# Two side streams of a scan kernel: from a flush at each pair's end to running on across it

## The chip, the cores and the metric

The kernel runs on one core of one Trainium2 chip. The metric is the device time of one execution in microseconds (us), the median of several runs. PE is TensorE, DVE is VectorE, ACT is ScalarE, POOL is GpSimd, SP is SyncE, which here issues all DMAs.

## The reference

64 images of 96 x 28 x 28 go through four layers in sequence.

```python
x = _L0_conv_ref(x, ...)      # expand to 576, depthwise 5x5 with four mixed experts per image, gate, project
x = _L1_conv_ref(x, ...)      # norm, in_proj, 3x3 conv, four-way selective scan, norm, gate, out_proj, MLP
t = _to_tokens(x)
t = t + _L2_attn_ref(_ln_t(t), ...)   # FFT over the 784 tokens, mixing, inverse FFT
t = t + _L2_ffn_ref(_ln_t(t), ...)    # quantised MLP
t = t + _L3_attn_ref(_ln_t(t), ...)
t = t + _L3_ffn_ref(_ln_t(t), ...)
x = _from_tokens(t, x)
```

The part that sets the order of everything is the scan in layer 1. For each of four directions k, 192 channels and 16 states, along 784 positions:

```python
def step(hst, inp):
    dt_t, x_t, B_t, C_t = inp
    dA = jnp.exp(dt_t[..., None] * A[None])
    dBx = dt_t[..., None] * B_t[:, :, None, :] * x_t[..., None]
    hst = hst * dA + dBx
    y_t = jnp.einsum('bkdn,bkn->bkd', hst, C_t)
    return (hst, y_t)
```

## The kernel before

Images are worked in 32 pairs. All that a pair needs falls into three strands, and the program interleaves the strands of neighbouring pairs.

**The scan** is the main strand. A pair has 192 *units*, in 12 blocks of 16. A block is a direction k and a channel tile T (T = 0 and 1: 128 channels of one image; T = 2: the remaining 64 of both). The order of the blocks is (0,0), (2,0), (0,1), (2,1), (0,2), (2,2) and then the same with k = 1 and 3. A unit holds 32 channels by 4 states on 128 partitions, along 784 positions. It consists of:
- `decay`: ACT computes da = exp(dt A), issued four units ahead (AHEAD, L74; the pool of da has 5 buffers);
- `spread_b`: PE spreads four rows of B to pb in PSUM, whenever image or group of states changes (4 times in a block with T = 0 or 1, 8 times with T = 2);
- `recur`: DVE multiplies pb by u to pd (L1045) and scans da and pd to h (L1050 forward, L1052 backward);
- POOL multiplies h by the rows of C (tile cs);
- `collect`: every four units, PE adds the four products into yp; at the end of a forward and backward block pair `keep` copies yp to xy, and SP stores it.

`prepare_block` fetches the next block's B rows (unit 1 of a block) and its dt4 and u4 (units 7 and 9 to 15, five buffers of each name), each spread to 128 partitions by the DMA; `fetch_c` fetches cs three units ahead (three buffers). All of them read DRAM tensors that the first stream wrote.

**Stream a** (`first_half`) is a generator that makes a pair's scan inputs: layer 0, then in_proj and the 3x3 convolution, then for k = 0 and 2 the B and C rows, dt and u, and after that (the point `ready`) the same for k = 1 and 3. **Stream b** (`second_half`) takes a pair's y through the rest of layer 1 and through layers 2 and 3. A generator yields after each *piece*. `yield 0` lets it go on in the same *window*, `yield 1` ends the window. A stream opens at most one window a unit, and `after(n, ...)` puts work off by n windows. Stream a has 131 windows, stream b 153.

The program order is written at build time by `run`. For each unit it writes the scan's instructions and then calls `advance`, which writes pieces of the due streams as long as the planner's clock of PE (`Clocks`, a table of assumed costs) is not past an allowance. That allowance is the planner's clock of DVE plus ROOM (0.3; EARLY, -0.3, where a new pb is two units off), plus GAIN (0.2) times how many windows the stream is behind its plan, plus a catch-up term that grows towards the end of the pair:

```python
late.update({v: v.base + (n + 1 - v.start) * v.rate - v.window for v in streams})      # L1179
advance(due, lambda v: until + GAIN * late[v] + max(0, late[v] - (per - n) / 4))      # L1182
if n == per - 1:
    finish(streams)
```

While the scan of pair p runs, stream a of pair p + 1 goes from unit 0 to unit 191, and stream b of pair p - 1 from unit 6 to unit 191. `finish` writes everything that is left of both after unit 191, without an allowance. So each stream begins and ends with a scan's pair. Each of the two streams has one PSUM bank; where one of them is alone (`alone`, in the first and last pair) it takes both in turn. After the last unit, `finish` writes all of the last pair's stream b. Each engine runs its instructions in the order written.

Of the kernel before, what the change touches and what calls it, by code (L numbers as in the profile page):

```python
# [75 lines left out]


BEFORE, ROOM, EARLY, GAIN, CHOICE = 6, 0.3, -0.3, 0.2, 0.1
WINDOWS = {"a": 131, "b": 153}


class Clocks:
# [107 lines left out]
class Stream:  # L190


    def __init__(self, name, clocks, pieces, rate, start):
        self.name, self.clocks, self.pieces = name, clocks, pieces
        self.window, self.later = 0, {}

        self.base, self.start, self.rate = 0, start, rate
# [27 lines left out]
class Model:  # L225
# [294 lines left out]
    def first_half(self, p, st):  # L520
        nc, act = self.nc, self.act
        after = lambda n, run: self.a_stream.after(n, run)
        dma = nc.sync.dma_start
# [7 lines left out]
        for i, k in enumerate((k0, k1)):  # L531
            t = k[:, : 10 * C]
# [223 lines left out]
        for b in range(2):  # L756
            v = wp[:, 4 * b : 4 * b + 4, :]
# [4 lines left out]
        for b in range(2):  # L762
            for h in range(2):
# [7 lines left out]
                v = xs[b][:, cols(h)]  # L771
# [121 lines left out]
        def project(k):  # L893
            v, s = self.rows_a.tile([128, L], F32, name="o"), stacked[k // 2]
            hi, mid, lo = parts
            for h in range(2):
                pt = bank()
                for T in range(3):
                    self.mm(
                        pt[:100, :HALF], w_p[:, k, T, :], source[T][:, cols(h)], start=(T == 0), stop=(T == 2)  # L900
                    )
                    if T == 1:
                        yield 0
                act(v[:100, cols(h)], pt[:100, :HALF], AF.Copy)
                if h == 0:
                    yield 1

            def placed(i, t):
                dma(st["b"][k][32 * i : 32 * i + 32], t[:32])
                dma(s[36 * i : 36 * i + 36], t[32:68])  # L910

            def second():
                act(mid, v[:68], AF.Copy)

            def third():
                self.gpsimd.tensor_sub(lo, v[:68], mid)
                placed(1, mid)
                placed(2, lo)

            def first():  # L920
                self.gpsimd.tensor_sub(v[:68], v[:68], hi)
                dma(st["c"][k % 2][32 * (k // 2) : 32 * (k // 2) + 32], v[68:100])
                placed(0, hi)

            act(hi, v[:68], AF.Copy)
            after(1, first)
            after(2, second)
            after(3, third)
            yield 1

        def product(k, T, dt, x):
            self.gpsimd.tensor_mul(us[0], dt, x)
            dma(st["dt"][k][T], dt)
            after(1, lambda: dma(st["u"][k][T], us[0]))

        def steps(k):

# [44 lines left out]
    def prepare_block(self, u, at):  # L982

        nc, st, k, T = self.nc, u["st"], u["k"], u["T"]
        if at == 1:
            if u["blk"] in (0, 1, 6, 7):
                self.bs[k] = self.bss.tile([C, L], BF16, name="bsl")
                nc.sync.dma_start(self.bs[k], st["b"][k])
        for name, v, when in (("dt4", "dt", (7, 10, 11, 12)), ("u4", "u", (9, 13, 14, 15))):
            if at in when:  # L990
                j = when.index(at)
                t = self.reps.tile([128, L], F32, name=name)
                self.landed[(u["p"], u["blk"], name, j)] = nc.sync.dma_start(
                    t, st[v][k][T][32 * j : 32 * j + 32, None, :].broadcast_to([32, 4, L])
                )
                self.rep[(u["p"], u["blk"], name, j)] = t

    def fetch_c(self, u):
        b = self.image_of(u)
        t = self.css.tile([128, L], F32, name="cs")  # L1000
        at = 32 * (u["k"] // 2) + 16 * b + 4 * u["g"]
        self.nc.sync.dma_start(t, u["st"]["c"][u["k"] % 2][at : at + 4].partition_broadcast(32))
        self.cs[self.key(u)] = t
# [80 lines left out]

    def run(self):
        nc, act, clocks = self.nc, self.act, self.clocks
        sts = [dict(p=p) for p in range(self.npairs)]
# [5 lines left out]

        fresh = lambda i: 0 < i < len(units) and self.key(units[i]) != self.key(units[i - 1])

        def stream(name, p, start=0):
            pieces = self.first_half if name == "a" else self.second_half
            v = Stream(name, clocks, pieces(p, sts[p]), WINDOWS[name] / (per - 2 - start), start)
            setattr(self, name + "_stream", v)
            return v  # L1100

# [20 lines left out]
        first, setup = stream("a", 0), Stream("b", clocks, self.setup_second(), 1, 0)  # L1122
# [3 lines left out]
        first.base, first.rate = first.window, 1  # L1126
        for at in range(16):
            self.prepare_block(units[0], at)
        self.fetch_c(units[0])
# [2 lines left out]
        decayed = AHEAD  # L1132
        clocks.dve = max(clocks.dve, clocks.pe)
        self.spread_b(units[0])
        streams = [first]
        for i in range(len(units) + 6):
            u = units[i] if i < len(units) else None
            n = i % per

            if u and n == 0:  # L1140
                self.alone = i // per in (0, self.npairs - 1)
            if i < per and first.over and streams == [first]:
                streams = [stream("a", 1, n)]
            elif u and n == 0 and i > 0:
                streams = [stream("a", i // per + 1, n)] if i // per + 1 < self.npairs else []
            elif u and n == 6 and i // per > 0:
                streams.append(stream("b", i // per - 1, n))
            if i % 4 == 2 and 6 <= i < len(units) + 3:
                self.collect(units[i - 6 : i - 2])
            if u:  # L1150
# [37 lines left out]
    def second_half(self, p, st):  # L1188
# [509 lines left out]
```

## Time and profile before

| | |
|---|---|
| median of 3 runs | 22441.52 us (22433.54 to 22450.66) |
| the profiled execution, its own time | 22503.17 us |
| its span, first to last instruction | 22501.5 us |
| mean granted clock of TensorE | 0.832 |
| busy: PE, DVE, ACT, POOL | 77%, 82%, 61%, 71% of the span |
| DMA | 4285.68 MB, 190 GB/s, 62.0% of the 16 engines' span |
| first scan starts, last scan starts | 415.9 us, 22173.4 us |

How to read it: busy times are of one profiled execution. A row of a group gives the line, the engine, the operation, output and inputs, shapes and count; then the busy time in us and the mean of one in ns; then the idle time of the engine just before these instructions and what ended most of it. The granted clock is the share of full speed that TensorE was allowed. L157 is the line of all ACT calls, L253 of all matmuls, L137 of the streams' DVE and POOL calls, so that the tile names tell the pieces apart: `slot` and `bank_b` belong to stream b; `r`, `k`, `t`, `o`, `pad`, `bank_a` to stream a.

### The profile page before, as it was taken

To read this page: it belongs to the slowest core of one execution; us is meant where nothing else is said; L and a number is where in the kernel's file an instruction comes from. 1 tells how busy PE (TensorE), PEld (TensorE's weight loads), DVE (VectorE), ACT (ScalarE), POOL (GpSimd) and SP (SyncE) were. 2 spreads that over 40 slices of the span, in tenths; PEclk is the share of its full clock that TensorE was granted. 3 is DMA by queue.
4 is the path that set the end of the run, shared out by engine and by line. 5 is a ranking of instruction groups with operands and counts; after the bars stand their busy time and mean duration, and the time that the engine had idled before them with its cause. 6 is when DMAs were issued, how large, how long until landed. Compare 5 with 4: busy or idle time off the path is not lost. (4 is left out here: it accounts for less than half of the span.)

```text
span 22501.5 us, 294265 instructions
## 1 busy us (share of the span) xinstructions
PE 17323.6 (77%) x100890; PEld 6770.9 (30%) x100890; DVE 18393.0 (82%) x15290; ACT 13649.8 (61%) x19357; POOL 15987.8 (71%) x9834
## 2 busy tenths in 40 slices
PE   5778777787777777777877777877778777778766
PEld 2233323332323333323323233323233232333222
DVE  2988888888888888888888888888888888888884
ACT  3566666666666666666666666666666666666654
POOL 2777777777777777777777777777777777777774
PEclk8888888888878888888888888888888888888877
DMA  5766666666666666666666666666666666666642
GB/s 155 229 189 197 201 203 187 191 193 200 202 194 187 189 195 198 205 192 192 192 196 200 193 189 197 196 197 200 193 191 190 195 202 193 193 193 190 199 158 63
DMA packets 1764775, 4285.68 MB, mean 190 GB/s; under 512 B 212500, under 2 KB 447084, under 8 KB 1763177
## 3 DMA queue, kind: packets, MB, share of 16 engines
q1 hardware_dynamic: 1763276, 4266.86, 62.0%
q8 instruction: 799, 13.09, 0.2%
q14 instruction: 700, 5.73, 0.1%
HBM read 3207.28 MB, written 882.92 MB: 182 GB/s over the span
## 5 line engine op out<-in xcount | busy, mean ns | idle before, releaser
L137 POOL TENSOR_TENSOR h<-h,cs 128x784 f32<-128x784 f32 x6144 | 11357.7, 1856 | 3875.7 <-DVE h L1050 1175.6
L1045 DVE TENSOR_TENSOR pd<-pb,u 128x784 f32<-128x784 f32 x6144 | 6016.4, 979 | 2346.6 <-PE pb L253 1029.1
L157 ACT ACTIVATE da<-dt,c_A_logs 128x784 f32<-128x784 f32 x6144 | 5661.2, 940 | 2014.4 <-DVE h L1052 865.4
L1052 DVE TENSOR_TENSOR_SCAN h<-da,pd 128x784 f32<-128x784 f32 x3072 | 5487.5, 1786 | 152.9 <-DVE pd L1045 2.8
L1050 DVE TENSOR_TENSOR_SCAN h<-da,pd 128x784 f32<-128x784 f32 x3072 | 5487.4, 1786 | 130.5
L253 PE MATMUL bank_a<-k,t 128*32 128x392 f32 (+1 forms) x37840 | 3984.7, 529 | 204.3 <-ACT pad L157 122.9
L253 PE MATMUL yp<-h,c_gather 128*32 128x512 f32 (+1 forms) x24576 | 3058.3, 595 | 131.3 <-POOL h L137 121.4
L137 POOL TENSOR_TENSOR slot<-slot,slot 96x392 f32<-96x392 f32 (+6 forms) x1700 | 2203.4, 1301 | 1197.3 <-ACT slot L157 988.8
L157 ACT ACTIVATE slot<-bank_b 128x392 f16<-128x392 f32 (+4 forms) x2546 | 1245.4, 489 | 2277.4 <-PE bank_b L253 2235.4
L253 PE MATMUL pb<-bsl,c_sel 96*128 96x512 bf16 (+1 forms) x4096 | 1192.2, 378 | 1320.4 <-DVE pd L1045 1294.1
L253 PEld LDWEIGHTS bank_a<-k,t 128*32 128x32 f32 (+1 forms) x37840 | 1267.2, 116 | 2391.1 <-issue 1894.3
L253 PEld LDWEIGHTS yp<-h,c_gather 128*32 128x32 f32 x24576 | 797.2, 124 | 2472.3 <-issue 2032.4
L253 PE MATMUL bank_b<-slot,c_center 96*128 96x392 f32 x1736 | 955.3, 638 | 396.1 <-DVE slot L137 243.8
L253 PE MATMUL bank_b<-c_fwd,slot 99*96 99x196 f32 (+1 forms) x3968 | 844.7, 359 | 354.1 <-DVE slot L137 254.9
L253 PEld LDWEIGHTS <-c_sel 96*128 96x128 bf16 x4096 | 353.5, 103 | 2469.8 <-issue 1666.9
L157 ACT ACTIVATE o<-bank_a,bn_b,bn_s 128x392 f32<-128x392 f32 x572 | 385.1, 673 | 1113.1 <-PE bank_a L253 1113.1
L157 ACT ACTIVATE slot<-slot 96x786 f32<-96x786 f32 (+5 forms) x1166 | 890.0, 790 | 85.9 <-DMA slot<-in_dt_w 37.6
L253 PEld LDWEIGHTS bank_b<-c_fwd,slot 99*96 99x96 f32 x3968 | 664.9, 175 | 583.4 <-issue 483.1
L157 ACT ACTIVATE slot<-bank_b,c_l_mix 96x393 f32<-96x393 f32 x736 | 446.1, 638 | 632.5 <-PE bank_b L253 418.0
L137 POOL TENSOR_TENSOR k<-k,r 128x784 f32<-128x784 f32 x256 | 472.0, 1844 | 423.1 <-ACT k L157 276.4
L253 PE MATMUL bank_a<-k,cv_diag 96*32 96x392 f32 x4464 | 612.2, 683 | 207.6 <-DMA k<-padded 175.8
L253 PE MATMUL bank_a<-k,k 108*128 108x392 bf16 x744 | 331.2, 445 | 567.5 <-ACT k L157 203.2
(265 smaller groups left out, 20797.5 us busy)
## 6 DMA issues: line engine op xcount, KB each, us to landing
cs<-crow SPq DMA_DIRECT2D x2048, 392.0 KB
dt<-dt SPq DMA_DIRECT2D x1536, 392.0 KB
u<-u SPq DMA_DIRECT2D x1536, 392.0 KB
k<-padded SPq DMA_DIRECT2D x2304, 256.0 KB
padded<-pad SPq DMA_DIRECT2D x384, 592.0 KB
u<-k SPq DMA_DIRECT2D x384, 392.0 KB
k<-padded SPq DMA_DIRECT2D x576, 224.0 KB
out<-o SPq DMA_DIRECT2D x288, 392.0 KB
```

The lines of the kernel that those rows point to most:

```text
L137: return run(out, *args, **kw)
L157: return self.nc.scalar.activation(out, in_, func, **kw)
L253: return self.nc.tensor.matmul(out, weights, moving, **kw)
L1045: self.awaited(nc.vector.tensor_mul(pd[:, :L], self.pb[:, :L], self.rep[(u["p"], u["blk"], "u4", u["j"])]), inputs)
L1050: scan = nc.vector.tensor_tensor_scan(h, da, pd[:, :L], 0.0, ALU.mult, ALU.add)
L1052: scan = nc.vector.tensor_tensor_scan(h[:, ::-1], da[:, ::-1], pd[:, L - 1 :: -1], 0.0, ALU.mult, ALU.add)
```

## The change

The two streams are no longer tied to a pair of the scan. A stream of the next pair begins when the one before it is over and its place in the plan has come: stream a of pair p + 1 not before the scan of pair p, stream b of pair p not before unit 6 of pair p + 1. The plan (`windows`) has stream a of pair p start at unit 8 of pair p - 1, reach its window 113 (`ready`) at unit 168 and end at unit 8 of pair p; stream b of pair p starts at unit 6 of pair p + 1 and ends 192 units later. `finish` after unit 191 is gone, and so is the catch-up term. As stream a may now be unfinished when the scan of its pair starts, it notes in `made` which B rows, C rows, dt and u it has written, and the scan's fetches call `require`, which writes windows of stream a without an allowance until the wanted one is there. In the built program this happens once a pair, for the B rows of k = 0 at unit 177, in pairs 4 to 31.

```diff
-WINDOWS = {"a": 131, "b": 153}
+A_WINDOWS, A_READY, B_WINDOWS = 131, 113, 153
+A_START, B_START = 8, 6
...
                 placed(1, mid)
                 placed(2, lo)
+                st["made"].add(("b", k))
...
             dma(st["dt"][k][T], dt)
-            after(1, lambda: dma(st["u"][k][T], us[0]))
+            st["made"].add(("dt", k, T))
+            def second():
+                dma(st["u"][k][T], us[0])
+                st["made"].add(("u", k, T))
+            after(1, second)
...
             if u["blk"] in (0, 1, 6, 7):
+                self.require(u["p"], ("b", k))
                 self.bs[k] = self.bss.tile([C, L], BF16, name="bsl")
...
                 j = when.index(at)
+                self.require(u["p"], (v, k, T))
                 t = self.reps.tile([128, L], F32, name=name)
...
     def fetch_c(self, u):
         b = self.image_of(u)
+        self.require(u["p"], ("c", u["k"]))
...
-        def finish(streams):
-            while any(not v.over for v in streams):
-                advance([v for v in streams if not v.over], lambda v: math.inf)
...
+        def windows(v, i):
+            if v is first and not i // per:
+                return first.base + i + 1
+            if v.name == "b":
+                return (i - (v.p + 1) * per - B_START) * B_WINDOWS / per
+            t = i - (v.p - 1) * per - A_START
+            ready = per - 24 - A_START
+            if t < ready:
+                return t * A_READY / ready
+            return A_READY + (t - ready) * (A_WINDOWS - A_READY) / (per - ready)
+
+        def require(p, key):
+            while key not in sts[p]["made"]:
+                v = self.a_stream if not self.a_stream.over else stream("a", self.a_stream.p + 1)
+                advance([v], lambda v: math.inf)
...
-            if u and n == 0:
-                self.alone = i // per in (0, self.npairs - 1)
-            if i < per and first.over and streams == [first]:
-                streams = [stream("a", 1, n)]
-            elif u and n == 0 and i > 0:
-                streams = [stream("a", i // per + 1, n)] if i // per + 1 < self.npairs else []
-            elif u and n == 6 and i // per > 0:
-                streams.append(stream("b", i // per - 1, n))
+            a, b = self.a_stream, self.b_stream
+            if a.over and a.p + 1 < self.npairs and a.p <= i // per:
+                a = stream("a", a.p + 1)
+            p = b.p + 1 if b else 0
+            if (b is None or b.over) and p < self.npairs and i >= (p + 1) * per + 6:
+                b = stream("b", p)
+            streams = [v for v in (a, b) if v and not v.over]
+            self.alone = i < per or a.over
...
-                late.clear(); late.update({v: v.base + (n + 1 - v.start) * v.rate - v.window for v in streams})
+                late.clear(); late.update({v: windows(v, i) - v.window for v in streams})
                 until = clocks.dve + (EARLY if fresh(i + 2) else ROOM)
-                due = [v for v in streams if not v.over and (v.open or late[v] > -BEFORE)]
-                advance(due, lambda v: until + GAIN * late[v] + max(0, late[v] - (per - n) / 4))
-                if n == per - 1:
-                    finish(streams)
-        finish([stream("b", self.npairs - 1)])
+                due = [v for v in streams if v.open or late[v] > -BEFORE]
+                advance(due, lambda v: until + GAIN * late[v])
+        while self.b_stream.p < self.npairs - 1 or not self.b_stream.over:
+            b = self.b_stream if not self.b_stream.over else stream("b", self.b_stream.p + 1)
+            advance([b], lambda v: math.inf)
```

More of the change, by code (lines that the diff above doesn't have):

```diff
@@ L190, with __init__ @@
 class Stream:
-    def __init__(self, name, clocks, pieces, rate, start):
-        self.name, self.clocks, self.pieces = name, clocks, pieces
+    def __init__(self, name, clocks, pieces, p=0):
+        self.name, self.clocks, self.pieces, self.p = name, clocks, pieces, p
         self.window, self.later = 0, {}
-        self.base, self.start, self.rate = 0, start, rate
         self.ready = False
@@ L922, in first @@
                 dma(st["c"][k % 2][32 * (k // 2) : 32 * (k // 2) + 32], v[68:100])
+                st["made"].add(("c", k))
                 placed(0, hi)
@@ L1086, in run @@
         nc, act, clocks = self.nc, self.act, self.clocks
-        sts = [dict(p=p) for p in range(self.npairs)]
+        sts = [dict(p=p, made=set()) for p in range(self.npairs)]
         self.rep, self.cs, self.bs, self.done, self.stored = {}, {}, {}, None, None
@@ L1094, in run, with stream @@
         fresh = lambda i: 0 < i < len(units) and self.key(units[i]) != self.key(units[i - 1])
-        def stream(name, p, start=0):
+        def stream(name, p):
             pieces = self.first_half if name == "a" else self.second_half
-            v = Stream(name, clocks, pieces(p, sts[p]), WINDOWS[name] / (per - 2 - start), start)
+            v = Stream(name, clocks, pieces(p, sts[p]), p)
             setattr(self, name + "_stream", v)
@@ L1115, in run @@
         late = {}
-        def finish(streams):
-            while any(not v.over for v in streams):
-                advance([v for v in streams if not v.over], lambda v: math.inf)
-        first, setup = stream("a", 0), Stream("b", clocks, self.setup_second(), 1, 0)
+        def windows(v, i):
[12 more added lines that the diff above has]
+                advance([v], lambda v: math.inf)
+        self.require = require
+        first, setup = stream("a", 0), Stream("b", clocks, self.setup_second())
         while not (first.ready and setup.over):
@@ L1125, in run @@
             self.alone = setup.over
-        first.base, first.rate = first.window, 1
+        first.base = first.window
         for at in range(16):
@@ L1134, in run @@
         self.spread_b(units[0])
-        streams = [first]
+        self.b_stream = None
         for i in range(len(units) + 6):
```

## The prediction

> **What bounds the kernel now.** I read the page first (who is busy), then the groups of VectorE, then one pair cut into its twelve blocks, then the waits of two of these stretches, then the timeline at the start of a pair.
>
> ```profile
> span 22501.5 us, 294265 instructions
> ...
> PE 17323.6 (77%) x100890; PEld 6770.9 (30%) x100890; DVE 18393.0 (82%) x15290; ACT 13649.8 (61%) x19357; POOL 15987.8 (71%) x9834
> ...
> L1045 DVE TENSOR_TENSOR pd<-pb,u 128x784 f32<-128x784 f32 x6144 | 6016.4, 979 | 2346.6 <-PE pb L253 1029.1
> L1052 DVE TENSOR_TENSOR_SCAN h<-da,pd 128x784 f32<-128x784 f32 x3072 | 5487.5, 1786 | 152.9 <-DVE pd L1045 2.8
> ```
>
> VectorE is the fullest engine. Each of the 6144 units costs it 979 + 1786 ns, and where nothing is late two scans start 2.84 us apart. Its idle time stands almost wholly ahead of the multiply L1045, that is, a product pb, an u or a free pd is late. The scans start at 415.9, pair 1 at 1009.8, pair 31 at about 21580, the last scan at 22173.4, and 328.5 us follow it. So the 30 pairs 1 to 30 take (21580 - 1009.8) / 30 = 685.7 us each.
>
> Pair 10 (7160 to 7854) by blocks of 16 units; the edges are the starts of every sixteenth scan in the timeline. Columns: window, its length, busy time of PE, PEld, DVE, ACT and POOL, granted clock, DMA share, GB/s.
>
> ```profile
> 7160.00:7221.00 61.00, 34.04 (x125) 11.34 (x124) 46.40 (x39) 39.91 (x61) 44.22 (x27) 0.67 0.65 228
> 7221.00:7274.00 53.00, 48.09 (x292) 17.02 (x291) 47.75 (x39) 21.63 (x35) 30.81 (x18) 0.94 0.73 181
> 7274.00:7331.00 57.00, 48.06 (x319) 15.29 (x318) 49.27 (x44) 32.07 (x43) 39.76 (x25) 0.91 0.70 212
> 7331.00:7378.00 47.00, 38.47 (x268) 12.52 (x264) 44.66 (x33) 31.73 (x41) 37.56 (x23) 0.93 0.68 202
> 7378.00:7431.00 53.00, 45.79 (x321) 15.20 (x320) 47.44 (x40) 37.34 (x48) 31.55 (x20) 0.94 0.70 206
> 7431.00:7485.00 54.00, 46.41 (x362) 20.01 (x366) 44.95 (x34) 27.63 (x39) 51.26 (x33) 0.91 0.76 231
> 7485.00:7538.00 53.00, 46.57 (x392) 22.58 (x381) 50.04 (x46) 36.97 (x52) 42.91 (x29) 0.97 0.67 197
> 7538.00:7594.00 56.00, 43.91 (x241) 18.25 (x240) 50.02 (x49) 26.73 (x37) 33.56 (x23) 0.82 0.50 164
> 7594.00:7647.00 53.00, 39.78 (x145) 13.46 (x144) 46.64 (x37) 39.39 (x63) 35.57 (x24) 0.71 0.45 141
> 7647.00:7712.00 65.00, 48.88 (x289) 18.01 (x288) 45.71 (x36) 38.63 (x52) 50.16 (x32) 0.74 0.67 196
> 7712.00:7783.00 71.00, 55.32 (x264) 31.36 (x263) 51.78 (x47) 48.42 (x74) 51.03 (x34) 0.83 0.52 175
> 7783.00:7854.00 71.00, 49.55 (x161) 16.50 (x160) 48.94 (x43) 47.35 (x71) 50.94 (x30) 0.65 0.56 185
> ```
>
> The reader is to see that VectorE's work is nearly the same in every block (573.6 in all, 47.8 each) and its idle time (length less DVE) is not: 14.6 in block 0, then 5.3, 7.7, 2.3, 5.6, 9.1, 3.0, 6.0, 6.4 in blocks 1 to 8 (45.2, or 5.65 each), then 19.3, 19.2, 22.1 in the last three. Of 120.4 us idle, 75.2 lie in four blocks around the end of the pair. Who was late, in blocks 1 to 8 and in blocks 9 to 11 (total, times, longest):
>
> ```profile
> DVE pd L1045 <- PE pb L253: 7.3, 6, 4.3
> ```
>
> ```profile
> DVE pd L1045 <- PE pb L253: 31.1, 10, 5.9
> ```
>
> A new pb is made whenever image or group changes: 4 times in a block of T = 0 or 1, 8 times where T = 2 (64 a pair; the page's 4096 pb matmuls / 2 / 32). So 40 spreads of the middle wait 0.18 us each and 20 of the end 1.56. pb stands on PE's queue behind the pieces that the plan placed ahead of it. The worst single wait is at unit 3 of the pair:
>
> ```profile
> 7173.61 0.92 POOL L137 TENSOR_TENSOR slot<-slot,slot 96x392 f32<-96x392 f32 x1 [0.86 <-ACT slot L157]
> ...
> 7176.39 2.82 PE L253 MATMUL yp<-h,c_gather 128*32 128x512 f32 x10 [2.24 <-POOL h L137]
> ...
> 7180.19 0.98 DVE L1045 TENSOR_TENSOR pd<-pb,u 128x784 f32<-128x784 f32 x1 [9.56 <-ACT xy L157]
> ```
>
> The flush at unit 191 has put the rest of both streams into ACT's, PE's and POOL's queues. A POOL addition of the old b stream waits for ACT, the multiplications h by cs stand behind it, the collecting matmuls wait for those, and pb behind these ends at 7179.98. The two scans around it stand 12.3 to 12.4 us apart in pairs 5, 10 and 20 alike.
>
> **The change part by part.**
>
> *No flush, no catch-up.* No arithmetic is added or taken away; the built programs hold the same instructions in another order. I counted pieces between one pd and the next in both orders (means of pairs 5 to 24, both streams together). Before: 20, 29, 27, 30, 29, 35, 26, 36, 42, 42, 40, 67 by block, 17 of them in unit 191 and none in units 0 to 3. After: 36, 35, 32, 34, 32, 39, 35, 31, 44, 41, 33, 32, two in unit 191, one or two in every unit around it. So the heap at the end goes for certain. What comes back in the middle?
> - Reading 1: a block of some 35 pieces idles like the middle does now, 5.65. Blocks 6 to 8 speak for it: 26 to 42 pieces, streams as late by the plan as they will always be afterwards, 5.1 us idle each. 12 x 5.65 = 67.8 instead of 120.4: 52.6 saved.
> - Reading 2: idle time grows evenly with the pieces. From 31.75 pieces and 5.65 us (blocks 1 to 8) to 49.7 pieces and 20.2 us (9 to 11) is 0.81 us a piece; 35.3 pieces then cost 8.5 us, 12 x 8.5 = 102: 18.4 saved, which is block 0's excess over its 20 pieces and little more.
>
> I see no ground to prefer one, and take the middle, 35.5 of 120.4 us, or 29.5%. Over all 30 pairs the idle time is 685.7 - 573.8 (DVE busy 17777.9 from 1009.8 to 22173, less 563.6 in pair 31, over 30) = 111.9 a pair; 29.5% of it is 33.
>
> *Data just in time.* Before, the B rows of the next pair's first block are made 12 units ahead of their fetch, its dt 16, its u 17. After, stream a is later: its demand for B fires at unit 177 of nearly every pair (pairs 4 to 31) and does two windows of a at once, dt is made 3 units ahead (3 x 2.84 = 8.5 us), u also 3. Behind a fetch that waits on SP stand cs, the other dt and u fetches and the streams' own DMAs; cs is fetched three units ahead, da four. The nearest row is ACT's wait for fetched dt: 407.4 us in 86 waits, longest 13.3. So between nothing and 13.3 us a pair; below nothing is excluded, since data are only made later. bsl has 14 units until pb needs it and dt4 five until da does, so I take 2.
>
> *Banks and end.* "alone" (either bank for one stream) holds as before in pair 0, and in pair 31 once stream a is over: nothing for pair 0. Pair 31 gets the rest of stream a and some of b (676 ACT instructions after its start instead of 627); pairs 1 and 2 have 40 and 10 fewer. I set these against each other, at nothing. Four more of b's pieces stand behind the last scan: 217 instead of 213, 328.5 x 4 / 213 = 6 us.
>
> *The sum.* 30 x (33 - 2) = 930 less, 6 more: span 22501.5 - 924 = 21577.5. The profiled execution took 22503.17 (1.7 outside the span), 61.65 above the median of 22441.52. On the median: 22441.5 - 924 = **21,518, say 21,520**.
>
> *The clock.* The granted clock is 0.91 to 0.97 in blocks 1 to 6, where PE's queue is dense, and 0.65 to 0.83 in the last three. Pieces that leave the end for the middle meet the better clock, so I charge nothing for it. The Trainium skill (TensorE: Matmul & The Clock Gate, "What's actually happening") speaks against this: half rate is the default and only a busy window of about 3.4 us lifts it, so a thinner stream of matmuls could run at half rate everywhere. By that rule, with block 11's 0.65 everywhere, the 273.4 us of PE in blocks 1 to 6 would become 273.4 x 0.93 / 0.65 = 391 us in 317 us of span, some 74 us a pair more, and the sum would be near 23,700. Block 3, the thinnest of these rows, still has 0.93, which is against it.
>
> **The rivals.**
> 1. *Only the flush goes.* Block 0's excess over the middle (14.6 - 5.65 = 9) and the pb wait after unit 191 (5.4) go; the catch-up's cost returns spread over the middle, which gets 35 pieces a block instead of 32. 14.4 x 0.93 = 13 a pair, 390 in all: 22,050, and with the late data at half their bound (6.7 a pair, 200 in all) 22,250. For it: block 5 idles 9.1 with 35 pieces. Against: block 8 has 42 and idles 6.4.
> 2. *No change.* The streams' pace of one pair in 192 units sets the time, and each settles so late that the stalls are the old ones: 22,440. For it: in the built order both streams now run 10 to 18 windows late all the time. Against: the measured stalls lie where the catch-up stands.
> 3. *Slower: permanent lateness.* GAIN x lateness (0.2 x 10 to 18) lets pieces in 2 to 3.6 us ahead at every unit, so that every spread waits as those of blocks 9 to 11 do now. 64 x 1.56 = 100, and other idle time at the middle's rate, (45.2 - 7.3) / 8 x 12 = 57: 157 instead of 120.4, x 0.93 is 34 more a pair, 1,010 in all: 23,450. It decides from (120.4 - 57) / 64 = 1.0 us a spread. Against: blocks 6 to 8 have about that lateness, and none of their spreads waits.
>
> **How the numbers follow.** The forecast (20,980 to 22,000) 0.52; rival 1 0.22; rival 2 0.07; rival 3 0.17; faster than 20,980, 0.02. 20,980 is reading 1 with nothing for the late data (52.6 x 0.93 = 48.9, x 30 = 1,467, less 6). Reading 2 with 13.3 for the data gives (17.1 - 13.3) x 30 - 6 = 108 less, 22,333. Rival 2 lies above it, so the range is 20,950 to 22,490 and leaves out 0.19. About 0.2% (45 us) is what a measurement tells from no change. Faster 0.52 + 0.22 + 0.02 = 0.76, same 0.07, slower 0.17.
>
> **What would show it.** Right: pairs of some 655 us; no wait of 9 us at unit 3; the last three blocks below 60 us each; pb waits below 1 us a spread; DVE busy near 85% of the span. Wrong: blocks 1 to 8 longer by what the end gave (rival 1 or 2); pb waits in all blocks (rival 3); ACT's da waiting for dt<-dt by more than 407 us in all (late data); a granted clock well below 0.83.

## The result, and the profile after

The changed kernel takes 22550.37 us (median of 4, 22520.44 to 22579.28) against 22438.79 us for the kernel before (4 runs, 22433.54 to 22450.66): a ratio of 1.0049, 95% interval 1.0031 to 1.0066. It is **slower by half a per cent**, little but clear of the noise, where 21,520 us was forecast; the time is 60 us above the upper end of the range. The profiled execution of after took 22540.4 us, 10 below its median, and that of before 64 above its own, so the two traces differ by only 37 us and show only that much of the 112 us between the medians.

The page of the changed kernel, rows as those shown of before (L1055 is the multiply that was L1045, L1062 the scan that was L1052, L252 the matmuls, L138 the streams' calls on DVE and POOL, L158 ACT):

```profile
span 22538.6 us, 294296 instructions
...
PE 17263.6 (77%) x100890; PEld 6918.3 (31%) x100890; DVE 18655.0 (83%) x15290; ACT 13610.6 (60%) x19358; POOL 15970.6 (71%) x9834
...
L1055 DVE TENSOR_TENSOR pd<-pb,u 128x784 f32<-128x784 f32 x6144 | 6015.0, 979 | 1675.7 <-PE pb L252 919.1
L1062 DVE TENSOR_TENSOR_SCAN h<-da,pd 128x784 f32<-128x784 f32 x3072 | 5487.6, 1786 | 139.3 <-PE bank_b L252 0.9
```

Two things stand in these rows. The idle time ahead of the multiply fell by 671 us, which is the gain the change was made for. And DVE's busy time rose by 262 us with the same 15290 instructions, which the prediction had held constant. The rest of the gain went to waits ahead of DVE's other instructions.

A *steady pair* below is the mean of pairs 5 to 24, taken between the starts of their first scans in the trace: 686.3 us before, 690.7 after. By blocks of 16 units, from the same scan starts:

| block | 0 | 1 | 2 | 3 | 4 | 5 | 6 | 7 | 8 | 9 | 10 | 11 |
|---|---|---|---|---|---|---|---|---|---|---|---|---|
| before | 60.8 | 52.9 | 56.2 | 46.7 | 51.5 | 53.4 | 53.4 | 55.7 | 52.7 | 64.8 | 70.1 | 68.0 |
| after | 50.3 | 46.8 | 69.7 | 64.8 | 50.2 | 53.7 | 57.2 | 51.7 | 58.0 | 63.0 | 62.9 | 62.2 |

Blocks 0, 1 and 9 to 11 together gave 31.4 us a pair, 14.7 of them in the last three. Blocks 2 and 3 took 31.6 back, blocks 6 and 8 another 9; blocks 4, 5 and 7 gave 5. In a steady pair the multiply's idle time fell from 73.5 to 52.5 us, while that of two groups of stream b, a scaling (slot<-bank_b,c_on,slot) and a norm step (bank_b<-bank_b,slot), rose from 11.2 to 28.9. Pair 10 of the changed kernel in the same cut and columns as before (window, length, busy time of PE, PEld, DVE, ACT, POOL, granted clock, DMA share, GB/s), the blocks that moved:

```profile
7148.00:7199.00 51.00, 32.13 (x130) 11.25 (x131) 47.19 (x40) 37.19 (x52) 44.05 (x25) 0.80 0.57 184
7199.00:7246.00 47.00, 24.65 (x102) 6.44 (x103) 44.66 (x34) 36.39 (x57) 41.38 (x26) 0.73 0.71 247
7246.00:7312.00 66.00, 49.09 (x184) 21.07 (x182) 48.75 (x42) 31.93 (x50) 39.76 (x24) 0.75 0.55 176
7312.00:7378.00 66.00, 54.11 (x390) 17.55 (x390) 50.27 (x45) 27.34 (x38) 38.79 (x25) 0.92 0.67 175
...
7709.00:7774.00 65.00, 47.99 (x258) 22.39 (x257) 50.15 (x39) 38.09 (x51) 46.73 (x27) 0.76 0.62 193
7774.00:7834.00 60.00, 44.75 (x219) 23.82 (x217) 51.89 (x43) 35.76 (x55) 47.14 (x33) 0.81 0.54 174
```

Block 0 now idles 3.8 us (14.6 before), but block 2 idles 17.3 (7.7) and block 3 15.7 (2.3). In the last three blocks the waits put down to pb are half of the 31.1 us shown of before, and a longer one stands beside them:

```profile
DVE pd L1055 <- PE pb L252: 15.3, 5, 6.0
DVE pd L1055 <- ACT o L158: 9.1, 1, 9.1
```

The second is most likely a wait for pb as well: it stands at unit 159 in each of pairs 5 to 24, 9 to 10 us long, and in 16 of these 20 it is put down to pb. So most of the waiting for pb in these blocks is still there.

What fills blocks 2 and 3 is in the timeline of pair 10. In the built order stream a now opens at unit 27 and stream b at unit 30 of a pair, 13 and 19 windows behind the plan (before: units 4 and 6, less than 3 windows behind), so the pieces behind their openings come faster and meet otherwise. In pair 10 of before, stream a's eight wide matmuls and stream b's first reductions also stood in the same units (15 to 22), but stream a's 5x5 convolution began at unit 23, five units ahead of stream b's first scaling; now it begins at unit 48, in the midst of the scalings (46 to 51):

```profile
7266.76 5.22 PE L252 MATMUL bank_a<-k,t 128*128 128x384 f32 x8 [0.92 <-ACT r L158]
...
7278.00 0.98 DVE L1055 TENSOR_TENSOR pd<-pb,u 128x784 f32<-128x784 f32 x1 [6.07 <-PE pb L252]
...
7292.80 1.18 DVE L138 SCALAR_TENSOR_TENSOR bank_b<-bank_b,slot 128x392 f32<-128x392 f32 x2 [6.33 <-ACT slot L158]
...
7319.15 2.84 PE L252 MATMUL bank_a<-k,t 128*32 128x392 f32 x16 [7.89 <-DMA k<-padded]
...
7325.63 0.63 DVE L138 SCALAR_TENSOR_TENSOR slot<-bank_b,c_on,slot 128x392 f32<-128x392 f32 x1 [11.38 <-PE bank_b L252]
7326.18 0.97 DVE L1055 TENSOR_TENSOR pd<-pb,u 128x784 f32<-128x784 f32 x1
```

At unit 39, pb stands behind stream a's eight wide mixing matmuls and stream b's first reductions. These eight took 2.8 us in every steady pair of before, at a granted clock of 1.00; here they take 5.2 at 0.54 (4.2 to 5.5 us at 0.50 to 0.67 over the steady pairs). At unit 42, a step of stream b's first norm waits on DVE for ACT, and the multiply waits behind it. At unit 48, PE stands 7.9 us at matmuls of a whose copies (eight DMAs issued from 7305.73) have not landed; b's matmuls queue behind these, DVE's scaling (slot<-bank_b,c_on) waits 11.4 us for them, and the multiply after it, which lacked nothing, starts when the scaling is done. Over the steady pairs units 39, 42 and 48 run 5.9, 10.0 and 11.2 us over the 2.84 of an unhindered unit, where those of before ran none over it: 27 of the 31.6.

### The profile page after: what moved, and what is told of

It reads as the page before. It is cut to its first block, busy times and chain, and to the rows that moved or that the text cites. A ratio compares the mean times of both kernels' runs of the same rounds, so it can differ in the third digit from the quotient of the medians.

```text
span 22538.6 us, 294296 instructions
## 1 busy us (share of the span) xinstructions
PE 17263.6 (77%) x100890; PEld 6918.3 (31%) x100890; DVE 18655.0 (83%) x15290; ACT 13610.6 (60%) x19358; POOL 15970.6 (71%) x9834
## 5 line engine op out<-in xcount | busy, mean ns | idle before, releaser
L138 POOL TENSOR_TENSOR h<-h,cs 128x784 f32<-128x784 f32 x6144 | 11354.2, 1857 | 4186.2 <-DVE h L1060 1425.2
L1055 DVE TENSOR_TENSOR pd<-pb,u 128x784 f32<-128x784 f32 x6144 | 6015.0, 979 | 1675.7 <-PE pb L252 919.1
L158 ACT ACTIVATE da<-dt,c_A_logs 128x784 f32<-128x784 f32 x6144 | 5671.1, 939 | 1158.5 <-DVE h L1062 512.5
L1062 DVE TENSOR_TENSOR_SCAN h<-da,pd 128x784 f32<-128x784 f32 x3072 | 5487.6, 1786 | 139.3 <-PE bank_b L252 0.9
L252 PE MATMUL bank_a<-k,t 128*32 128x392 f32 (+1 forms) x37840 | 3987.6, 519 | 477.0 <-DMA k<-padded 234.1
L252 PE MATMUL yp<-h,c_gather 128*32 128x272 f32 (+1 forms) x24576 | 3153.9, 594 | 202.6 <-POOL h L138 202.1
L138 POOL TENSOR_TENSOR slot<-slot,slot 96x392 f32<-96x392 f32 (+6 forms) x1700 | 2207.3, 1304 | 1288.9 <-ACT slot L158 1060.1
L158 ACT ACTIVATE slot<-bank_b 128x392 f16<-128x392 f32 (+4 forms) x2538 | 1239.4, 488 | 2334.2 <-PE bank_b L252 2273.1
L252 PE MATMUL pb<-bsl,c_sel 96*128 96x512 bf16 (+1 forms) x4096 | 1166.2, 371 | 1347.5 <-DVE pd L1055 1289.4
L252 PEld LDWEIGHTS bank_a<-k,t 128*32 128x32 f32 (+1 forms) x37840 | 1367.5, 117 | 2598.3 <-issue 2122.9
L252 PEld LDWEIGHTS yp<-h,c_gather 128*32 128x32 f32 x24576 | 809.4, 123 | 2539.6 <-issue 1857.6
L252 PE MATMUL bank_b<-slot,c_center 96*128 96x392 f32 x1736 | 915.8, 614 | 335.0 <-DVE slot L138 245.3
L252 PEld LDWEIGHTS <-c_sel 96*128 96x128 bf16 x4096 | 348.3, 102 | 2409.6 <-issue 1268.8
L252 PE MATMUL bank_b<-c_fwd,slot 99*96 99x196 f32 (+1 forms) x3968 | 897.3, 375 | 230.7 <-DVE slot L138 140.5
L158 ACT ACTIVATE o<-bank_a,bn_b,bn_s 128x392 f32<-128x392 f32 x572 | 386.6, 676 | 1116.1 <-PE bank_a L252 1115.9
L158 ACT ACTIVATE slot<-slot 96x786 f32<-96x786 f32 (+5 forms) x1166 | 889.4, 789 | 83.9 <-DMA slot<-in_dt_w 37.7
L158 ACT ACTIVATE slot<-bank_b,c_l_mix 96x393 f32<-96x393 f32 x752 | 457.9, 642 | 767.1 <-PE bank_b L252 587.2
L252 PEld LDWEIGHTS bank_b<-c_fwd,slot 99*96 99x96 f32 x3968 | 703.6, 186 | 525.8 <-issue 360.6
L252 PE MATMUL bank_a<-r,c_exp_w 96*64 96x392 f32 (+1 forms) x1218 | 559.2, 623 | 300.8 <-ACT pad L158 201.9
L252 PE MATMUL bank_a<-k,k 108*128 108x392 bf16 x744 | 318.1, 428 | 587.7 <-DMA k<-dt_parts 279.8
L252 PE MATMUL bank_b<-c_inv,slot 99*96 99x394 f32 x2016 | 752.9, 517 | 13.2 <-ACT slot L158 13.1
```

Source lines behind the costliest of these rows:

```text
L138: return run(out, *args, **kw)
L158: return self.nc.scalar.activation(out, in_, func, **kw)
L252: return self.nc.tensor.matmul(out, weights, moving, **kw)
L1055: self.awaited(nc.vector.tensor_mul(pd[:, :L], self.pb[:, :L], self.rep[(u["p"], u["blk"], "u4", u["j"])]), inputs)
L1062: scan = nc.vector.tensor_tensor_scan(h[:, ::-1], da[:, ::-1], pd[:, L - 1 :: -1], 0.0, ALU.mult, ALU.add)
```

## Why: the theories, and the experiments

**Theory 1**: the heap's gain came as predicted, and it was lost at places where the new order lets engines collide, the streams' openings and the maximum (below) above all. **Theory 2**: the plan's feedback sets the sum of the stalls; take one away, and the streams gain or lose lateness until others make it up. **Theory 3**: the openings are hurried because both streams start late. **Theory 4**: the allowance is too small for the lateness that it lets build up; more constant ROOM and less lateness is better. **Theory 5**, formed after the first of these runs: every order of the pieces has its own sum of stalls, and no one quantity of the plan orders them. It forecasts a spread and no time, so a run can speak for it only by falling where the others do not. Times are medians of 2 to 10 executions, ratios are to the kernel before.

### The maximum of two SBUF tiles

DVE's extra 262 us stand in one row, which grew by 277: stream b's maximum of two SBUF tiles, eight a pair. The group in the trace of before, then of after:

```profile
L137 DVE TENSOR_TENSOR slot<-slot 96x393 f32<-96x393 f32 x256 | 184.4, 720 | 0.0
```

```profile
L138 DVE TENSOR_TENSOR slot<-slot 96x393 f32<-96x393 f32 x256 | 461.3, 1802 | 0.0
```

In a steady pair it went from 5.8 to 15.7 us. One takes 0.54 us when POOL is free. When a POOL multiplication is running it is held until that ends, or one or two more that follow it, and the profile counts the wait as busy (the longest: 5.4 us after, 6.1 us before). The timeline of pair 10, POOL's two multiplications of 1.83 us and the maximum that starts 0.78 us after the first of them:

```profile
7765.65 3.66 POOL L138 TENSOR_TENSOR h<-h,cs 128x784 f32<-128x784 f32 x2
...
7766.43 3.30 DVE L138 TENSOR_TENSOR slot<-slot 96x393 f32<-96x393 f32 x1
...
7769.66 0.97 DVE L1055 TENSOR_TENSOR pd<-pb,u 128x784 f32<-128x784 f32 x1
```

POOL is done at 7769.31, the maximum at 7769.73. In the trace of after, all 109 maxima that started while nothing ran on POOL took 0.54 to 0.56 us, and all 129 that took over 0.7 us ended 0.42 to 0.43 us after the end of a POOL instruction. The Trainium skill (SBUF — State Buffer, "SBUF: two separate sides") has the rule: VectorE and GpSimd share a pair of ports, a VectorE instruction with two SBUF inputs and a GpSimd instruction that reads SBUF exclude each other for a whole instruction. These rows agree. The scan and the multiply have only one input in SBUF (pd and pb are PSUM tiles) and are not held: the scan takes 1785 to 1790 ns each time, with POOL busy during two thirds of it.

First in two kernels, the maximum was replaced by two scalar_tensor_tensor that read one operand from PSUM; ACT's eight Abs a pair go with it, and the planner's clocks and the order of the rest are kept.

```diff
-            act(zi, pi, AF.Abs, scale=di)
...
             def first(...):
...
+                nc.vector.scalar_tensor_tensor(zi, pi, di, zr, ALU.mult, ALU.max)
+                nc.vector.scalar_tensor_tensor(zi, pi, negd, zi, ALU.mult, ALU.max)
...
-                self.vector.tensor_tensor(zi, zi, zr, ALU.max)
```

In the changed kernel:

> The changed kernel, in the same order, with VectorE's max of two SBUF tiles (zi, zr in the attention; 8 a pair, 0.72 us each before the change and 1.80 us after it) replaced by two scalar_tensor_tensor that take one operand from PSUM (0.62 us each, 16 a pair), and ScalarE's 8 Abs left out. Theory 1 (what the end of the pair gave is lost to places where the new order lets engines collide, this max with GpSimd among them): 16 x 0.62 = 9.9 us instead of 15.7 a pair, about 180 us less than the changed kernel in all, 22370, and no such instruction over 0.8 us. Theory 2 (the plan's feedback keeps the stalls: what is saved in one place is waited for in another): within 50 us of the changed kernel's 22550.

Measured: 22392.4 us, ratio to before 0.9968 (0.9955 to 0.9981); steady pair 685.0 (-5.7), DVE busy 578.0 (-5.2), no block moved by more than 3 us; theory 1 had said 22370. The same in the kernel before:

> The kernel before with the same replacement. There the max was hardly held up (0.72 us), so both theories expect no gain: theory 1 9.9 instead of 5.8 us of VectorE a pair, 130 us more, 22570; theory 2 within 50 us of 22440.

Measured: 22456.15 us, 0.9999 (0.9989 to 1.0008); steady pair 684.3 (-2.0), although the two instructions cost 9.9 where the maximum cost 5.8, for which theory 1 had expected 130 us more. What made up for it is idle time ahead of the scaling by c_l_mix, which fell from 12.1 to 5.9; that the missing Abs did this is likely, but no run separates it. The new rows of the changed kernel show no wait any more:

```profile
L1437 DVE SCALAR_TENSOR_TENSOR slot<-bank_b,l_negd,slot 96x393 f32<-96x393 f32 x240 | 149.6, 623 | 8.5
```

It follows that the maximum's wait is a cost of its own and a good part of what the change lost; with it out of both, the changed kernel is the faster one by 64 us, or 0.3%. It is not the larger part of the missing gain.

### The openings

Stream b, planned to open at unit 54 or 102 instead of 6:

```diff
-A_START, B_START = 8, 6
+A_START, B_START = 8, 54
...
-            if (b is None or b.over) and p < self.npairs and i >= (p + 1) * per + 6:
+            if (b is None or b.over) and p < self.npairs and i >= (p + 1) * per + B_START:
```

> The changed kernel with stream b's plan and start 48 units later (B_START 54), so that stream a starts at unit 33 and stream b at unit 85 of a pair instead of 27 and 30. About 38 more of b's windows then stand behind the last scan, some 80 us. Theory 1 (the two streams' openings collide in blocks 2 and 3): blocks 2 and 3 fall from 67 us to under 58 each and the steady pair from 690.7 to 665 or less, the whole to about 21900. Theory 2 (feedback): the steady pair stays within 685 to 695, the stalls stand elsewhere, the whole is 22500 to 22650.

Measured: 23135.09 us, 1.0299 (1.0279 to 1.0319). Blocks 2 and 3 fell from 134.5 to 112.0 as theory 1 has it, but blocks 1, 5, 8 and 11 rose to 56.6, 63.6, 64.1 and 73.0: steady pair 708.1, and 399.5 us behind the last scan instead of 330.3. Neither theory had a pair that long. In the built order the demand for B rows at unit 177 now writes five windows of stream a at once where it wrote two, which may be part of block 11's.

> The changed kernel with stream b 96 units later (b begins at unit 133, a at 34): a third place of the two streams against each other. Theory 1 (only the coincidence of the openings costs): blocks 2 and 3 below 115, the steady pair 670 or less. Theory 2: the steady pair 685 to 710 with the worst waits at other units. Some 76 more of b's windows stand behind the last scan (about 160 us).

Measured: 23585.14 us, 1.05 (1.0479 to 1.0521); blocks 2 and 3 at 111.0 together, steady pair 721.1, 477.7 behind the last scan. Again blocks 2 and 3 fall as theory 1 has it, and the pair as neither has it.

Three more windows between the copies of stream a and the matmuls that read them, for the wait of unit 48:

```diff
-A_WINDOWS, A_READY, B_WINDOWS = 131, 113, 153
+A_WINDOWS, A_READY, B_WINDOWS = 134, 116, 153
...
         fetch_copies(1)
         dg = taps(0)
+        yield 1
+        yield 1
+        yield 1
         yield 1
```

> The changed kernel with three more empty windows of stream a between the fetch of the first shifted copies and the first 5x5 convolution that reads them (A_WINDOWS 134, A_READY 116). Theory 1 (at unit 48 PE stands 7.9 us for these copies, with stream b's matmuls, VectorE's scaling of them and the scan's multiply queued behind): the 14.7 us between two scans there goes, the wait of the scaling for PE falls from 16 to about 6 us a pair, 10 us a pair and 300 in all, to 22250. Theory 2 (feedback): within 60 us of 22550.

Measured: 22815.44 us, 1.016 (1.0141 to 1.0179); steady pair 700.2. The scaling's group, 486.9 us idle in the changed kernel, became

```profile
L138 DVE SCALAR_TENSOR_TENSOR slot<-bank_b,c_on,slot 128x392 f32<-128x392 f32 x186 | 113.3, 609 | 124.5 <-PE bank_b L252 120.3 <-DMA slot<-slot 2.2 <-DMA k<-padded 2.0
```

so that wait is gone (16.4 to 3.6 us a pair), and blocks 2 and 3 take 135.8 all the same: other waits have come in its place (c_l_mix 7.0 to 16.5 a pair, the multiply 52.5 to 61.6). The edit does more than it was meant to: with three more windows to a pair, stream a opens at unit 31 of the built order and not at 27.

A plan that counts from the unit in which each stream really opens, so that no opening is late:

```diff
-            if v.name == "b":
-                return (i - (v.p + 1) * per - B_START) * B_WINDOWS / per
...
+            return (i + 1 - v.start) * (A_WINDOWS if v.name == "a" else B_WINDOWS) / 160
```

> The changed kernel with each stream's plan counted from the unit at which that stream really begins (131 or 153 windows in 160 units), and not from the calendar of the pair. No flush and no catch-up, as in the changed kernel; but a stream opens with no lateness, as in the kernel before, and not some 13 to 16 windows late. In the order written, a runs from unit 0 to 187 and b from 6 to 2. Theory 3 (the streams' openings in blocks 2 and 3 cost 134 instead of 103 us because they are hurried from their first piece): blocks 2 and 3 fall below 110 together, the steady pair below 672, the whole to about 22000. Theory 2 (feedback: the same number of pieces a unit gives the same stalls, wherever the plan puts them): the steady pair within 683 to 695, the whole 22400 to 22650.

Measured: 22629.24 us, 1.0074 (1.0058 to 1.0091). Blocks 2 and 3 came down to 96.9, below the 102.9 of before, as theory 3 expects of them; but with this plan the streams also open elsewhere (units 0 and 6), so the run does not tell hurry from place. Blocks 4 to 8 went from 271 to 308: the streams now become late there. Steady pair 690.5, as after, which is what theory 2 said. All four edits reached the wait they were aimed at, and not one of them made a pair shorter by as much as a microsecond.

### What the old end cost

The kernel before with the flush, without the catch-up term:

```diff
-                advance(due, lambda v: until + GAIN * late[v] + max(0, late[v] - (per - n) / 4))
+                advance(due, lambda v: until + GAIN * late[v])
```

> The kernel before without its catch-up term, but with the flush after unit 191: one half of the change alone. More is left for the flush. If the heap at the end is what costs, blocks 9 to 11 fall from 203 by 10 to 15 us and block 0 rises from 61 by 15 to 25 us, so that the steady pair is 690 to 700; theory 2, 683 to 695.

Measured: 22835.32 us, 1.0166 (1.0146 to 1.0187); steady pair 697.8. Now 51 pieces fall into unit 191, and the wait at unit 3, 9.56 us before, is

```profile
7272.11 0.98 DVE L1045 TENSOR_TENSOR pd<-pb,u 128x784 f32<-128x784 f32 x1 [40.74 <-ACT xy L157]
```

Block 0 rose from 60.8 to 93.0, and blocks 9 to 11 fell from 202.9 only to 185.2. So the catch-up cost about 18 us of the end, and a flush without it costs more than that. The rest of what makes these blocks long is neither flush nor catch-up: the changed kernel's 188.1 has it still, and the orders below do not all have it (170.7 with ROOM 0.8).

### The allowance

One constant, ROOM (and EARLY, always 0.6 less), which says how far ahead of DVE's planned clock the pieces may go:

```diff
-BEFORE, ROOM, EARLY, GAIN, CHOICE = 6, 0.3, -0.3, 0.2, 0.1
+BEFORE, ROOM, EARLY, GAIN, CHOICE = 6, 2.3, 1.7, 0.2, 0.1
```

> The changed kernel with a larger constant allowance (ROOM 2.3, EARLY 1.7), so that the streams keep their pace with some 10 windows less lateness; a then begins at unit 8 and b at unit 15. The lead that PE's pieces have over VectorE is about the same in sum, lateness alone is smaller. Theory 2 (the lead is what the pace needs): the steady pair 683 to 695. Lateness as such as the cause: below 675.

Measured: 22076.32 us, 0.9828 (0.9809 to 0.9848); steady pair 671.6. The kernel before with the same constants:

> The kernel before, flush and catch-up kept, with the larger constant allowance alone (ROOM 2.3, EARLY 1.7). Little is then left for the end of a pair. Theory 4 (the pace costs less where a constant allowance holds it than where lateness and catch-up hold it; whether the streams run across the pair's end matters little): the steady pair, 686, falls to 672 or less and the whole to 22000 or less, as with the same allowance in the changed kernel. Rival, theory 5 (every order of the pieces gives its own sum of stalls, and 672 was one draw): 675 to 700. If running across the end is what gains once the pace is easy: above 680, and more than 8 us over the changed kernel with this allowance.

Measured: 22177.26 us, 0.9872 (0.9857 to 0.9887); steady pair 675.2, at the edge of what theory 5 allows. So with ROOM 2.3 the change itself is worth 101 us *less* time, where with ROOM 0.3 it costs 112. Two values on either side, in the changed kernel (3.3, then 1.3):

> The changed kernel with ROOM 3.3, EARLY 2.7. Theory 4: the steady pair at or below that of ROOM 2.3, 660 to 672. Theory 5: anywhere from 665 to 710, with no order in ROOM.

> The changed kernel with ROOM 1.3, EARLY 0.7. Theory 4: between the changed kernel (691) and ROOM 2.3 (672), 676 to 686. Theory 5: anywhere from 665 to 710.

Measured: 22543.07 us, 1.0037 (1.0022 to 1.0053), and 22060.6 us, 0.9821 (0.9801 to 0.984). Then 0.8, 1.8 and 2.8:

> The changed kernel with ROOM 0.8, EARLY 0.2. The steady pair is 690.7, 671.1, 671.6 and 687.8 with ROOM 0.3, 1.3, 2.3 and 3.3. If the level of the allowance decides, this one lies on the line between: 677 to 685. If each order of the pieces gives its own sum, it may lie anywhere between 665 and 710.

> The changed kernel with ROOM 1.8, EARLY 1.2. If the level of the allowance decides: 665 to 674 a steady pair. If each order gives its own sum: anywhere between 665 and 710.

> The changed kernel with ROOM 2.8, EARLY 2.2. If the level of the allowance decides: 675 to 684 a steady pair. If each order gives its own sum: anywhere between 665 and 710.

Measured: 21741.63 us, 0.9685 (0.9663 to 0.9708); 22355.15, 0.9958 (0.9941 to 0.9975); 22421.75, 0.9988 (0.9977 to 0.9998). All seven, with the units at which the streams open in the built order and DVE's accounts in a steady pair:

| ROOM | 0.3 | 0.8 | 1.3 | 1.8 | 2.3 | 2.8 | 3.3 |
|---|---|---|---|---|---|---|---|
| stream a, b open at unit | 27, 30 | 23, 27 | 21, 26 | 20, 22 | 8, 15 | 7 to 13, 14 to 18 | 4, 10 |
| steady pair, us | 690.7 | 659.2 | 671.1 | 680.6 | 671.6 | 684.3 | 687.8 |
| DVE idle | 107.5 | 79.9 | 94.3 | 101.7 | 89.0 | 100.9 | 102.3 |
| the maximum | 15.7 | 12.7 | 10.2 | 11.5 | 15.3 | 16.2 | 18.8 |

More ROOM lets the streams open earlier, with one small exception, and the time does not follow: **theory 4 falls**. Every row has the same instructions, moved by a few units, and a pair of 659 to 691 us. Since a stream's period is a pair's, it stands at the same units of every pair (but for 2.8, where three places alternate), so one collision of 10 us costs 300. That is what theory 5 says, though its own range missed the 659.2.

One of the collisions can be followed through the table. PE's wait for the copies of stream a (unit 48 above) stands only in the orders where the 5x5 convolution begins in the midst of stream b's scalings or with the first of them: ROOM 0.3 (units 48, and 46 to 51; 6.7 us a pair), 1.8 (39, and 39 to 44; 9.6) and some pairs of 2.8 (4.3). With ROOM 0.8 (40, and 44 to 49), 1.3, 2.3 and 3.3 it begins three or four units ahead of them, and there is no such wait; block 3 idles 1.9 us with ROOM 0.8 and 15.2 with 0.3. At 0.8 and above the demand for B rows at unit 177 does not arise either. And the granted clock goes loosely with the time: 0.834 and 0.835 in the two slowest of the seven (3.3 and 0.3), 0.841 to 0.851 in the three fastest (0.8, 1.3, 2.3). Whether that is a cause or follows from fewer stalls, no run here tells.

The fastest, ROOM 0.8, by its page:

```profile
span 21747.2 us, 294632 instructions
...
PE 16971.2 (78%) x100890; PEld 6764.3 (31%) x100890; DVE 18561.8 (85%) x15290; ACT 13585.5 (62%) x19357; POOL 15972.5 (73%) x9834
...
L1055 DVE TENSOR_TENSOR pd<-pb,u 128x784 f32<-128x784 f32 x6144 | 6015.9, 979 | 1517.9 <-ACT slot L158 551.9
```

pb no longer leads the releasers of the multiply. Theory 2 also falls in its strict form, as the sum of the stalls is not held: it is 80 here and 107 there.

### Both findings together

The maximum taken out at three of these allowances (2.3, 1.3, 0.8), the edits as above:

> The changed kernel with ROOM 2.3 and the max taken from PSUM, both together. With ROOM 2.3 the max still takes 15.3 us of VectorE a pair, with the replacement 9.8: 5.5 less a pair, 170 in all, 21910 against 22076. By theory 2 or 5: within 50 us of 22076.

> ROOM 1.3 and the max taken from PSUM. With ROOM 1.3 the max takes only 10.2 us of VectorE a pair (15.7 in the changed kernel, 15.3 with ROOM 2.3), and the replacement 9.8. If waiting for GpSimd is what the replacement saves, it saves next to nothing here: 22000 to 22080, against 22061 without it. If it gains by something else (the 8 Abs that ScalarE no longer does), it gains here what it gained in the changed kernel, 150 us: about 21900.

> The changed kernel with ROOM 0.8 and EARLY 0.2 (the fastest order so far, 21,742 us) and the maximum of stream b made by two scalar_tensor_tensor with one operand in PSUM, in place of an Abs on ScalarE and a maximum of two SBUF tiles. If the maximum's wait is a cost of its own that adds to any order (the lock): its 12.7 us a pair become some 9.8, the steady pair 656 instead of 659.2, the time about 21,650 (21,600 to 21,700). If such an edit is again only another order with its own sum of stalls (theory 5): anything from 21,600 to 21,900, and the rest of VectorE's idle time moves by more than the maximum's own time.

Measured: 21868.35 us, 0.974 (0.9723 to 0.9756); 22076.12, 0.9831 (0.9813 to 0.985); 21668.9, 0.9659 (0.9642 to 0.9675), the fastest version of this study. The forecasts of a wait that stands for itself (21910, 22000 to 22080, 21,600 to 21,700) hold in the second and third, and the first gained 40 us more. The two instructions cost 9.9 a pair everywhere. What the maximum cost above that, and what the pair gave:

| kernel | after | ROOM 2.3 | ROOM 0.8 | ROOM 1.3 | before |
|---|---|---|---|---|---|
| maximum's time less 9.9 | 5.8 | 5.4 | 2.8 | 0.3 | -4.1 |
| pair shorter by | 5.7 | 8.1 | 3.3 | -1.0 | 2.0 |

In four of the five the pair gave what the instruction gave, within 3 us. The kernel before is the exception (the shorter wait of c_l_mix, above).

## Why the prediction was wrong, point by point

- *What bounds the kernel.* Right: VectorE at one unit per 2.84 us, and idle time ahead of the multiply.
- *The heap at the end goes.* Right in place, too large in size: the wait of unit 3 is gone, and blocks 0 and 1 gave 16.6 us a pair. But the last three blocks, which were to come below 60 us each, take 62 to 63: they still idle 38.3 us a pair (56.6 before), where the two readings left them 17 or 26. Most of their waiting for pb stands without flush and catch-up too (9 us at unit 159 alone).
- *What comes back in the middle: the step that failed.* I let 29.5% of the idle time go, between two readings of 18 and 53 us; it went from 112.4 to 107.5, or 4%. Both readings took the number of pieces in a block as what decides its stalls. Blocks 2 and 3 of after have 32 and 34 pieces and idle 20.9 and 15.2 us in a steady pair; block 8 has 44 and idles 8.0. Even the rows of before were against it: blocks 8 and 9 have 42 pieces each and idle 6.4 and 19.3. In blocks 2 and 3 it is decided by which pieces meet, as units 39, 42 and 48 show. Moving both streams by some 23 units, with 13 and 19 windows to make up from the first piece, laid stream a's convolution among b's scalings, and no count of pieces shows that. The built order would have.
- *DVE busy held at 573.8.* Wrong: in the steady pairs 573.8 became 583.2, 9.4 of the some 35 us by which a pair missed the forecast of 655. I had no row for it in what I read, but the group of the maximum (0.72 us for what takes 0.54 alone) stood in the trace of before and had its cause in it.
- *Data just in time, 2 us a pair, not below nothing.* Wrong in sign: ACT's wait for fetched dt fell from 407.4 to 166.8 us. Of the 12.7 us that a steady pair of before waited for dt, 11.2 stood in block 1, right behind the flush; block 1 of after has 1.1. I had excluded a gain because data are only made later. That the flush delayed their fetches is the obvious reason, but it is not shown: without the catch-up, with three times the pieces in the flush, block 1 waits 6.7 and not more.
- *Banks and end.* The 6 us behind the last scan were 2. Pairs 1 and 2, set at nothing, became 34 and 17 us shorter, which is why the trace loses only 37 us when pairs 3 to 30 lost 89 in all.
- *The clock at nothing.* Right on the whole, wrong in places: granted clock 0.832 and 0.835; TensorE spent 32.7% and 32.6% of the steady pairs at half rate. The feared fall by the Trainium skill's rule (TensorE: Matmul & The Clock Gate, "What's actually happening") did not come on the whole, though in block 1 of pair 10, where PE's work went from 48.1 to 24.7 us, the clock fell from 0.94 to 0.73, and in block 2 from 0.91 to 0.75. There the eight wide matmuls of unit 39 take 5.2 us instead of 2.8, so some 2.4 of the 6 us that the multiply waits behind them go with the clock (an estimate, the difference of the two).
- *The rivals.* Nearest was rival 2, no change, to which I gave 0.07; its ground was the lateness of 10 to 18 windows, and the openings do start 13 and 19 windows late. But the stalls are "the old ones" only in part (blocks 9 to 11); the others are new, at other units. Rival 3 is not what happened: the multiply's waits for pb fell from 1029.1 to 919.1 us.

What stays open: what an order's sum of stalls consists of could be read from its trace, never foretold. The kernel before was not run with ROOM 0.8, so what the change is worth there is not known, and whether ROOM 0.8 would stay best under another small change was not tried.

## What to carry to other kernels

Where a hand-written or planned order interleaves periodic streams, a change of the plan moves them against each other, and their collisions are a new draw: here the same instructions gave pairs of 659 to 691 us for steps of half a microsecond in one constant, more than the change that was being judged. So lay the built order beside the trace and look at what each long or late piece meets at its new place, and judge the idea over several neighbouring settings before keeping or dropping it. What came nearest to its forecast was to replace an instruction that was held up, the maximum: 3 to 8 us a pair where it had waited, and nothing where it had not (ROOM 1.3).

## What the runs showed of the hardware

VectorE's maximum of two fp32 SBUF tiles (96 x 393) took 0.54 us alone and up to 5.4 us in the trace of after (6.1 before) when it met GpSimd's instructions, and the profile books the wait as busy time, so that an engine's busy time depends on the order. A VectorE instruction of the same size with one operand in PSUM kept its 0.62 us in every order, and so did the scan its 1.79 us, which reads one tile from SBUF and one from PSUM.
